# A fused attention and feed-forward block: six of eight W1 blocks by seven products, and a new order of work around them

## The chip, the cores and the metric

The kernel runs on one core of one Trainium2 chip. The core has five engines, each with its own queue that it works through in order: TensorE (PE in the profile; PEld is its weight loads, which run beside its matmuls), VectorE (DVE), ScalarE (ACT), GpSimd (POOL) and SyncE (SP), which here only issues DMAs. The metric is the device time of one launch in microseconds (us): 1520.04 us, the median of three runs (1518.93 to 1522.97).

## The reference

Everything is float32. With x and ctx of shape (128 batches, 128 positions, 256 features), 16 heads of 16 features and a hidden layer of 1024:

```python
q = heads(x @ Wq + bq); k = heads(ctx @ Wk + bk); v = heads(ctx @ Wv + bv)
scores = q @ k^T / 4, and -1e30 where key position >= query position
attn = softmax(scores); the first query's row is zero
x1 = layer_norm(x + merge(attn @ v) @ Wo + bo) * ln1_g + ln1_b
out = layer_norm(x1 + relu(x1 @ W1 + b1) @ W2 + b2) * ln2_g + ln2_b
```

W1 is 256 x 1024 and W2 is 1024 x 256. The two of them are what the change is about.

## The kernel before, in words

Batches are worked in 64 pairs, numbered p. The program is written out in full, with no loop on the chip, and the order of the instructions in the source is the order in each engine's queue; a framework adds the semaphores. After some opening pairs (functions `third` to `sixth`) there are 57 calls of `step(p)`, for p = 7 to 63. One step holds work of several pairs at once: the weighing of the values for pair p-2, the scores and the softmax of pair p, the projections of pair p+1, the first norm of pair p-2, the W1 layer of pair p-3, the W2 layer of pair p-4 and the second norm of pair p-5. All steps but the last (56 of them) have the W1 layer done by `hidden_by_seven`.

"By seven" is a Strassen-like scheme: a product of 2 x 2 blocks takes seven block products where the plain way takes eight, and the rest is additions on other engines. `second_by_seven` (the W2 layer) does this for the whole layer: seven products of four matmuls each into two PSUM banks, py (bank 6) and pz (bank 7), with `empty`, which puts NOPs on TensorE's queue, after each matmul. `sum_of_seven` adds them on VectorE. `combine_hidden` (GpSimd, lines 795 to 798) makes the sums hS of hidden blocks that three of the products need.

For W1 the class `Hidden` does it for the first 2*NI of the eight blocks of 128 hidden units. NI is 2: four blocks by seven products (`run`, line 899, numbers 1 to 7), each of NI matmuls of 128 columns. Each product fills half a PSUM bank of 512 words; two share a bank (`WHERE`). The other four blocks are plain: `plain` (line 938), two matmuls of 256 columns for each. `combine_normed` (GpSimd, lines 866 to 869) makes the sums xS of the normed input, and `combine_w1` those of the weights, once.

The seven products become hidden blocks like this: `keep` (ACT, line 908) copies product 1, `u2` (DVE, line 911) adds 6, `u3` (lines 914 and 915) adds 7 and then 4, and `rest` adds 5 to all odd blocks (line 919) and 2 and 3 to the low halves (line 923). Then `relu` (ACT, line 928) works on each block, in place for those by seven and out of PSUM for the plain ones. Of the four in-place ones, blocks 2 and 3 are done at the head of the next step.

Other lines that matter: `weigh` (PE, lines 494 and 504, bank 7) opens a step, and `context` (ACT, line 516) copies its result out. `scores_both` (PE, line 384) follows and writes all eight banks; its last two groups go to banks 6 and 7, and its high part to banks 0 to 3. `mask` and `mask_high` (DVE, lines 398, 754, 758) find the maxima, `exponential_by_head` (ACT, line 775) does 32 exponentials. Then come `queries` (bank 4, copied at line 272), `attention_out` (bank 5, added at line 549), `keys` (bank 0, copied at line 291) and `values` (bank 1, copied by `spread_values`, line 315, and `stack_values`, line 324). `norm1` is line 565 and `norm2` line 602, both on ACT. `sums` takes reciprocals on DVE (line 433) and multiplies on GpSimd (line 434). `turn` (DVE, line 447) transposes a third of the softmax in blocks of 32, `bring` (SP, line 462) moves the blocks by 16 DMAs. `turn_x1` (DVE, line 674, and five DMAs) transposes x1. `deviation` and `shift` are small GpSimd operations (lines 543, 544, 588), `residual1` (lines 577, 580) and `finish` (lines 608, 609) larger ones.

Of the kernel before, what the change touches and what calls it, by code (L numbers as in the profile page):

```python
# [10 lines left out]
ALU = mybir.AluOpType  # L11
AX = mybir.AxisListType

P = 128
# [5 lines left out]
def tile_cross_attention_block(  # L20
# [22 lines left out]
    nc = tc.nc  # L43
# [30 lines left out]
    states = {}  # L74
# [135 lines left out]
    def at_bank(i, name):  # L210
        return psum.tile([P, 512], F32, tag=f"b{i}", name=name)
# [229 lines left out]
    def turn(p, hi, t):  # L441

        st = states[p]
        if "tb" not in st:
            st["tb"] = wide(f"tb_{p}").rearrange("p (j n) -> p j n", j=NS)
        at = (t if hi else 2) * 256
        nc.vector.transpose(  # L447
            st["tb"][:, :, at : at + 256].rearrange("p j (n a) -> p n j a", a=32),
            st["sm", hi].rearrange("p h j -> p (h j)")[:, t * 1024 : (t + 1) * 1024].rearrange(
                "p (n j a) -> p n j a", j=NS, a=32  # L450
            ),
        )
# [100 lines left out]
    def attention_stats(p):  # L553
        stats(p, states[p]["t1"], 1)
        deviation(p, 1)
# [42 lines left out]
    def norm2(p):  # L598
        st = states[p]
        t2, sd, nb = st["t2"], st["sd", 2], st["nb", 2]  # L600
        for s in range(2):
            nc.scalar.activation(
                t2[:, s], t2[:, s], AF.Identity, bias=nb[:, s], scale=sd[:, s]
            )
# [195 lines left out]
    def second_by_seven(p):  # L800

        st = states[p]
        hT, hs = st["hT"], st["hS"]
        py = st["py"] = at_bank(6, f"py_{p}")
        pz = st["pz"] = at_bank(7, f"pz_{p}")

        def product(out, left, right, after):
            for k in range(FC // 2):
                nc.tensor.matmul(  # L809
                    out, left(k), right(k), start=(k == 0), stop=(k == FC // 2 - 1)  # L810
                )
                empty(after // (FC // 2) + (after % (FC // 2) > k))

        def raw(e, s):
            return lambda k: hT[:, 2 * k + e, s * P : (s + 1) * P]

        def weights(e, h):
            return lambda k: w2[:, 2 * k + e, h * P : (h + 1) * P]

        product(py[:, :P], raw(0, 0), weights(0, 0), 7)  # L820
        product(pz[:, :P], raw(1, 0), weights(1, 0), 7)
        product(pz[:, 2 * P : 3 * P], raw(1, 1), lambda k: wt[:, 3, k], 7)
        product(py[:, 3 * P :], lambda k: hs[:, 0, k], lambda k: wt[:, 0, k], 7)
        product(py[:, 2 * P : 3 * P], lambda k: hs[:, 2, k], lambda k: wt[:, 2, k], 7)
        product(py[:, P : 2 * P], lambda k: hs[:, 1, k], lambda k: wt[:, 1, k], 7)
        product(pz[:, P : 2 * P], lambda k: hs[:, 3, k], weights(1, 1), 6)

    def sum_of_seven(p):

# [17 lines left out]
            t[:, :3], t[:, :3], pz[:, : 3 * P].rearrange("p (n d) -> p n d", d=P), ALU.add  # L847
        )

    NI = 2  # L850
    w1t = const.tile([P, 4, NI, P], F32, tag="w1t", name="w1t")

    def combine_w1():
# [7 lines left out]
    def combine_normed(p):  # L861

        st = states[p]
        x1T = st["x1T"]
        xs = st["xS"] = ffn.tile([P, 4, NS, 32], F32, tag="xS", name=f"xS_{p}", bufs=1)
        nc.gpsimd.tensor_tensor(xs[:, 0], x1T[:, 1, :, 0, :], x1T[:, 1, :, 1, :], ALU.add)
        nc.gpsimd.tensor_tensor(xs[:, 2], x1T[:, 0, :, 0, :], x1T[:, 1, :, 0, :], ALU.subtract)
        nc.gpsimd.tensor_tensor(xs[:, 1], xs[:, 0], x1T[:, 0, :, 0, :], ALU.subtract)
        nc.gpsimd.tensor_tensor(xs[:, 3], x1T[:, 0, :, 1, :], xs[:, 1], ALU.subtract)

    class Hidden:

        WHERE = {1: (2, 0), 6: (2, 1), 7: (3, 0), 4: (3, 1), 2: (4, 0), 3: (4, 1), 5: (5, 0)}

        def __init__(self, p):
            st = states[p]
# [2 lines left out]
            self.h = self.hT[:, : 2 * NI].rearrange("p (i e) (s t) -> p e s i t", e=2, s=2)  # L879
            self.banks, self.plains = {}, {}  # L880

        def of(self, which, n=1):
            at, n0 = self.WHERE[which]
            if at not in self.banks:
                self.banks[at] = at_bank(at, f"phs_{self.p}_{at}")
            return self.banks[at][:, n0 * NI * P : (n0 + n) * NI * P]

        def run(self, which):
            raw = lambda s, k: self.x1T[:, s, :, k, :]
# [24 lines left out]
            nc.vector.tensor_tensor(self.h[:, 1, 1], self.h[:, 1, 0], self.one(7), ALU.add)  # L914
            nc.vector.tensor_tensor(self.h[:, 0, 1], self.h[:, 1, 1], self.one(4), ALU.add)

        def rest(self):
            odd = self.hT[:, 1 : 2 * NI : 2].rearrange("p i (s t) -> p i s t", s=2)
            nc.vector.tensor_tensor(
                odd, odd, self.one(5)[:, :, None, :].to_broadcast([P, NI, 2, P]), ALU.add  # L920
            )
            low = self.h[:, :, 0]
            nc.vector.tensor_tensor(
                low, low, self.of(2, 2).rearrange("p (e i t) -> p e i t", e=2, i=NI), ALU.add
            )

        def relu(self, f):
# [395 lines left out]
    def hidden_by_seven(p):  # L1323

        h = Hidden(p - 3)
        h.run(1)
        h.run(6)
        h.keep()
        stack_values(p)
        h.u2()  # L1330
        h.run(7)
        h.run(4)
        h.u3()
        h.run(2)
        h.run(3)
        h.run(5)
        h.rest()
        norm2(p - 5)
        h.plain([4], 0)
        h.relu(4)  # L1340
        h.plain([5], 1)
        h.relu(5)
        h.plain([6], 2)
        h.relu(6)
        turn(p, 1, 1)
        h.plain([7], 0)
        h.relu(7)
        for f in range(NI):
            h.relu(f)
        states[p - 3]["rest"] = h  # L1350

    def step(p):
        last = p == NP - 1
        weigh(p - 2)
        context(p - 2)
        if p > 7:
            for f in range(NI, 2 * NI):
                states[p - 4]["rest"].relu(f)
        scores_both(p)
        combine_hidden(p - 4, POOL_ALONE)  # L1360
        add_bo(p - 1)
        if not last:
            combine_normed(p - 3)
            load_ahead(p)
        mask(p, 0, B)
        if last:
            mask(p, 0, A)
        mask_high(p, A)
        exponential_by_head(p, 1, ONES, True)
        mask_high(p, B)  # L1370
        exponential_by_head(p, 1, TWOS, True)
        if not last:
            mask(p, 0, A)
        low_maximum(p)
        if not last:
            exponential_by_head(p, 0, range(H), True)
            queries(p + 1)
        attention_out(p - 2)
        attention_sum(p - 2)
        attention_stats(p - 2)  # L1380
        shift(p - 2, 1)
        if last:
            values(p)
            values_out(p)
            stats(p - 5, states[p - 5]["t2"], 2)
            deviation(p - 5, 2)
            norm1(p - 2)
            exponential_by_head(p, 0, range(H), True)
        else:
            norm1(p - 2)  # L1390
            keys(p + 1)
            values(p)
        sums(p, 1, ONE)
        sums(p, 1, TWO)
        if p + 2 < NP:
            tokens(p + 2, "x")
            tokens(p + 2, "c")
        if last:
            shift(p - 5, 2)
            turn_x1(p - 2)  # L1400
        else:
            stats(p - 5, states[p - 5]["t2"], 2)
            scale_and_shift(p - 5)
        turn(p, 1, 0)
        second_by_seven(p - 4)
        if not last:
            sums(p, 0, ALL)
        residual1(p - 3)
        sum_of_seven(p - 4)
        if last:  # L1410
            sums(p, 0, ALL)
        if not last:
            turn_x1(p - 2)
            spread_values(p)
            hidden_by_seven(p)
        else:
            turn(p, 1, 1)
            hidden(p - 3, range(FC))
        turn(p, 0, 0)
# [15 lines left out]
    def behind(p):  # L1435

        weigh(p)
        context(p)
        if p == NP - 2:
            norm2(p - 4)  # L1440
            finish(p - 4)
            store(p - 4)
            bring(p + 1, nc.scalar, LATE_FIRST[len(EVERY) // 2 :])
        combine_hidden(p - 2, VECTOR_ALONE)
        if p == NP - 2:
            stats(p - 3, states[p - 3]["t2"], 2)
            scale_and_shift(p - 3)
        norm2(p - 3)
        finish(p - 3)
        store(p - 3)  # L1450
        second_by_seven(p - 2)
        attention_out(p)
        attention_sum(p)
        attention_stats(p)
        shift(p, 1)
        residual1(p - 1)
        sum_of_seven(p - 2)
        stats(p - 2, states[p - 2]["t2"], 2)
# [75 lines left out]
```

## Time and profile before

| what | value |
|---|---|
| median of three runs | 1520.04 us |
| the profiled execution, its own time | 1522.34 us |
| its span | 1520.5 us |
| granted TensorE clock | 0.998 |
| TensorE matmuls busy | 99% |
| weight loads / VectorE / ScalarE / GpSimd busy | 89% / 84% / 85% / 89% |

The rows of the timeline read: start in us, length in us, engine, line, operation, tile written <- tiles read, shape, how many were merged, and in brackets how long the engine sat idle before and what ended that. Every float32 matmul of the source shows as two records. The record of a matmul begins before the one ahead of it has ended, so that the spacing of starts tells its cost. A row of the windows view has the stretch, its length, and the busy time and instruction count of each engine in it.

### The profile page before, as it was taken

The page shows a single profiled execution, that of the slowest core. Times are in us where ns is not written, and L with a number is a line of the kernel's source. Part 1 is how long each engine was busy: PE and PEld are TensorE (multiplying, and loading weights), DVE is VectorE, ACT ScalarE, POOL GpSimd, SP SyncE. Part 2 cuts the span into 40 slices and gives each one's busy share as a digit, 9 for nine tenths or more (in the row PEclk, how much of TensorE's full clock was granted, in tenths as well). Part 3 has the DMA queues.
Part 4 walks back from the last instruction along what each step waited for, and adds up shares of the span by engine and source line. Part 5 has one row for each costly group of instructions (what it writes and reads, how often), then busy time and mean ns, then how long its engine had stood idle before and what let it go on. Part 6 is the DMA issues. An engine that isn't in the chain of part 4 may idle for free.

```text
span 1520.5 us, 53525 instructions
## 1 busy us (share of the span) xinstructions
PE 1506.5 (99%) x18598; PEld 1359.2 (89%) x18598; DVE 1281.6 (84%) x2607; ACT 1295.0 (85%) x5271; POOL 1358.2 (89%) x1510
## 2 busy tenths in 40 slices
PE   8999999999999999999999999999999999999998
PEld 7788998999999989989989999899899899999987
DVE  7989888888888888888888888888888888888775
ACT  5668988988988989989889889899899898898862
POOL 6878999999999999999999999999999999999983
PEclk9999999999999999999999999999999999999999
DMA  9456665655655656656566566556565666664441
GB/s 196 91 113 144 147 151 139 138 133 135 141 142 138 131 140 135 147 138 135 134 137 142 141 140 129 142 133 150 134 140 131 139 137 146 138 132 124 108 119 47
DMA packets 415314, 204.59 MB, mean 135 GB/s; under 512 B 282448, under 2 KB 383056, under 8 KB 415056
## 3 DMA queue, kind: packets, MB, share of 16 engines
q1 hardware_dynamic: 412768, 199.34, 56.9%
q8 instruction: 158, 2.59, 0.8%
q10 hardware_dynamic: 2288, 1.85, 0.5%
q14 instruction: 100, 0.82, 0.2%
HBM read 70.26 MB, written 33.29 MB: 68 GB/s over the span
## 4 chain that ended last, share of the span: by engine, by line
PE 92%; DVE 3%; ACT 2%; POOL 1%; DMA 1%; SPq 1%; issue 1%; ACTq 0%; POOLq 0%; DVEq 0%
PE ph L938 13%; PE py L809 13%; PE phs L899 11%; PE pz L809 10%; PE pq L261 7%; PE po L523 7%; PE pv L301 7%; PE pk L261 6%; PE pss L384 6%; PE pc L504 4%; PE ph L710 3%; PE pc L494 2%; ACT sm L775 1%; SPq L462 1%; POOL sm L434 1%
## 5 line engine op out<-in xcount | busy, mean ns | idle before, releaser
L775 ACT ACTIVATE sm<-pss,nmx 128x128 f32<-128x128 f32 x944 | 328.5, 405 | 87.1 <-POOL hS L795 74.9
L434 POOL TENSOR_TENSOR sm<-sm,rs 128x1024 f32<-128x1024 f32 x192 | 362.1, 1900 | 3.4 <-DVE rs L433 3.3
L447 DVE STREAM_TRANSPOSE tb<-sm 128x1024 f32<-128x1024 f32 x186 | 223.4, 1226 | 110.9 <-POOL sm L434 90.7
L775 ACT ACTIVATE sm<-sm,nmx 128x64 f32<-128x64 f32 x944 | 313.7, 404 | 0.0
L775 ACT ACTIVATION_READ_ACCUMULATOR sm<-sm,nmx 128x1 f32 x912 | 235.1, 258 | 0.0
L775 ACT ACTIVATION_READ_ACCUMULATOR sm<-pss,nmx 128x1 f32 x912 | 223.3, 245 | 0.0
L938 PE MATMUL ph<-x1T,w 128*128 128x256 f32 x896 | 213.8, 386 | 0.1
L938 PEld LDWEIGHTS ph<-x1T,w 128*128 128x128 f32 x896 | 161.3, 190 | 36.1 <-ACT vd L324 18.8
L809 PE MATMUL py<-wt,hS 128*128 128x128 f32 x1440 | 171.2, 275 | 1.0 <-DVE hS L796 0.5
L809 PEld LDWEIGHTS py<-wt,hS 128*128 128x128 f32 x1440 | 165.8, 192 | 1.4 <-DVE hS L796 0.7
L758 DVE TENSOR_REDUCE nmx<-pss 128x4 f32<-128x512 f32 x236 | 150.9, 680 | 0.0
L398 DVE TENSOR_TENSOR sm<-pss,neg 128x256 f32<-128x256 f32 (+1 forms) x276 | 108.3, 435 | 34.9 <-PE pss L384 32.0
L928 ACT ACTIVATE hT<-ph,b1e_c 128x256 f32<-128x256 f32 x224 | 98.8, 465 | 35.5 <-PE ph L938 35.5
L291 ACT ACTIVATE kT<-pk,bkh,half 128x256 f32<-128x256 f32 x252 | 123.7, 609 | 4.0 <-PE pk L261 4.0
L261 PE MATMUL pq<-xT,wq 128*128 128x256 f32 x504 | 125.4, 392 | 0.5 <-DVE sm L398 0.5
L523 PE MATMUL po<-wo,cxT 128*128 128x256 f32 x512 | 121.3, 380 | 0.7 <-ACT cxT L516 0.7
L301 PE MATMUL pv<-wv,cT 128*128 128x256 f32 x512 | 120.9, 379 | 0.0
L261 PE MATMUL pk<-cT,wk 128*128 128x256 f32 x504 | 119.2, 379 | 0.0
L795 POOL TENSOR_TENSOR hS<-hT 128x512 f32<-128x512 f32 x57 | 72.2, 1267 | 50.2 <-ACT hT L928 50.1
L523 PEld LDWEIGHTS po<-wo,cxT 128*128 128x128 f32 x512 | 96.9, 190 | 14.4 <-ACT cxT L516 1.2
L261 PEld LDWEIGHTS pq<-xT,wq 128*128 128x128 f32 x504 | 90.7, 189 | 20.8 <-issue 9.8
L301 PEld LDWEIGHTS pv<-wv,cT 128*128 128x128 f32 x512 | 97.2, 190 | 13.2
(164 smaller groups left out, 3987.4 us busy)
## 6 DMA issues: line engine op xcount, KB each, us to landing
pT<-tb SPq DMA_DIRECT2D x976, 96.0 KB, 2.2
x1t<-tbx SPq DMA_DIRECT2D x252, 64.0 KB, 1.8
x1T<-x1t SPq DMA_DIRECT2D x63, 256.0 KB, 2.9
out_dram<-t SPq DMA_DIRECT2D x63, 256.0 KB, 2.4
xb<-in_x_dram SPq DMA_DIRECT2D x124, 128.0 KB, 3.8
cb<-in_ctx_dram SPq DMA_DIRECT2D x124, 128.0 KB, 3.8
x<-in_x_dram SPq DMA_DIRECT2D x31, 512.0 KB, 4.6
w<-in_L_xattn_W_dram SPq DMA_DIRECT2D x2, 1024.0 KB, 7.7
```

What stands on the lines that cost most here:

```text
L261: nc.tensor.matmul(ps[:, m * TP : (m + 1) * TP], w[:, k, m * P : (m + 1) * P], src[:, k, :], start=(k == 0), stop=(k == KC - 1),)
L291: nc.scalar.activation(st["kT"][:, m, e, :], pk[:, m * TP : (m + 1) * TP], AF.Identity, bias=bkh[:, m, e : e + 1], scale=half[:, e : e + 1],)
L301: nc.tensor.matmul(pv[:, s * D : (s + 1) * D], st["cT"][:, k, s * P : (s + 1) * P], wv[:, k, :], start=(k == 0), stop=(k == KC - 1),)
L398: nc.vector.tensor_tensor(st["sm", hi][:, 4 * r : 4 * r + 4, :], st["sps", hi][r][:, : 4 * n].rearrange("p (n j) -> p n j", j=n), no[:, No ...
L434: nc.gpsimd.tensor_tensor(sm[:, part, :], sm[:, part, :], rs[:, :, None].to_broadcast([P, part.stop - part.start, n]), ALU.mult,)
L447: nc.vector.transpose(st["tb"][:, :, at : at + 256].rearrange("p j (n a) -> p n j a", a=32), st["sm", hi].rearrange("p h j -> p (h j)")[:, ...
L523: nc.tensor.matmul(po[:, s * D : (s + 1) * D], cxT[:, k, s, :], wo[:, k, :], start=(k == 0), stop=(k == KC - 1),)
L758: nc.vector.tensor_reduce(st["nmx", 1][:, 4 * r : 4 * r + 4], st["sps", 1][r].rearrange("p (n j) -> p n j", j=P), AX.X, ALU.max, negate=True,)
L775: nc.scalar.activation(sm[:, h, :], src, AF.Exp, bias=nmx[:, h : h + 1], scale=1.0, **({"accum_out": st["su", hi][:, h : h + 1]} if summed ...
L809: nc.tensor.matmul(out, left(k), right(k), start=(k == 0), stop=(k == FC // 2 - 1))
L899: nc.tensor.matmul(ps[:, i * P : (i + 1) * P].rearrange("p (n a) -> p n a", a=32), left(i), right, start=True, stop=True,)
L938: nc.tensor.matmul(self.plains[f].rearrange("p (s i a) -> p s i a", s=2, a=32), w1[:, k, f * P : (f + 1) * P], self.x1T[:, :, :, k, :], st ...
```

## The change

1. NI goes from 2 to 3: six of the eight W1 blocks are done by seven products, each of three matmuls of 128 columns, and only blocks 6 and 7 are plain. Each of the seven products has a bank of its own (banks 2, 3, 4, 5, 6, 0, 1), and the plain blocks reuse banks 2 and 3.
2. `rest` is split into `add2`, `add3` and `add5`, placed apart. The relus run in the order 0, 2, 4, 6, 1, 7, and 3 and 5 at the head of the next step. `norm1` moves behind `u3`, and the W1 function takes over `turn_x1`, which stood ahead of it.
3. On GpSimd the two high softmax products come first; `combine_normed`, `deviation` and `shift` of the first norm stand behind them.
4. On VectorE the second high transpose, which stood among the W1 work, moves to directly behind the first, ahead of the W2 sum.
5. The NOPs among the W2 matmuls become 5 for a product (4 for the last) in place of 7 (6).
6. In the closing pairs, `finish` and `store` of one pair move behind other GpSimd work.

```diff
-        product(py[:, :P], raw(0, 0), weights(0, 0), 7)
+        product(py[:, :P], raw(0, 0), weights(0, 0), 5)
...
-        product(pz[:, P : 2 * P], lambda k: hs[:, 3, k], weights(1, 1), 6)
+        product(pz[:, P : 2 * P], lambda k: hs[:, 3, k], weights(1, 1), 4)
...
-    NI = 2
+    NI = 3
...
-        WHERE = {1: (2, 0), 6: (2, 1), 7: (3, 0), 4: (3, 1), 2: (4, 0), 3: (4, 1), 5: (5, 0)}
+        WHERE = {1: 2, 6: 3, 7: 4, 4: 5, 2: 6, 3: 0, 5: 1}
...
-        def rest(self):
+        def add2(self):
+            nc.vector.tensor_tensor(self.h[:, 0, 0], self.h[:, 0, 0], self.one(2), ALU.add)
+
+        def add3(self):
+            nc.vector.tensor_tensor(self.h[:, 1, 0], self.h[:, 1, 0], self.one(3), ALU.add)
+
+        def add5(self):
             odd = self.hT[:, 1 : 2 * NI : 2].rearrange("p i (s t) -> p i s t", s=2)
             nc.vector.tensor_tensor(
                 odd, odd, self.one(5)[:, :, None, :].to_broadcast([P, NI, 2, P]), ALU.add
-            )
-            low = self.h[:, :, 0]
-            nc.vector.tensor_tensor(
-                low, low, self.of(2, 2).rearrange("p (e i t) -> p e i t", e=2, i=NI), ALU.add
             )
...
         h.u3()
+        norm1(p - 2)
         h.run(2)
+        h.add2()
         h.run(3)
         h.run(5)
-        h.rest()
-        norm2(p - 5)
-        h.plain([4], 0)
+        h.relu(0)
+        h.relu(2)
         h.relu(4)
-        h.plain([5], 1)
-        h.relu(5)
+        h.add3()
+        h.add5()
         h.plain([6], 2)
         h.relu(6)
-        turn(p, 1, 1)
-        h.plain([7], 0)
+        turn_x1(p - 2)
+        h.plain([7], 3)
+        norm2(p - 5)
+        h.relu(1)
         h.relu(7)
-        for f in range(NI):
-            h.relu(f)
...
         if p > 7:
-            for f in range(NI, 2 * NI):
-                states[p - 4]["rest"].relu(f)
+            states[p - 4]["rest"].relu(3)
+            states[p - 4]["rest"].relu(5)
...
         if not last:
-            combine_normed(p - 3)
             load_ahead(p)
...
-        attention_stats(p - 2)
-        shift(p - 2, 1)
+        stats(p - 2, states[p - 2]["t1"], 1)
...
-            norm1(p - 2)
             keys(p + 1)
             values(p)
         sums(p, 1, ONE)
         sums(p, 1, TWO)
+        if not last:
+            combine_normed(p - 3)
+            deviation(p - 2, 1)
+            shift(p - 2, 1)
...
         turn(p, 1, 0)
+        if not last:
+            turn(p, 1, 1)
         second_by_seven(p - 4)
...
-            turn_x1(p - 2)
             spread_values(p)
             hidden_by_seven(p)
...
         if p == NP - 2:
             norm2(p - 4)
-            finish(p - 4)
-            store(p - 4)
             bring(p + 1, nc.scalar, LATE_FIRST[len(EVERY) // 2 :])
         combine_hidden(p - 2, VECTOR_ALONE)
         if p == NP - 2:
             stats(p - 3, states[p - 3]["t2"], 2)
             scale_and_shift(p - 3)
+            finish(p - 4)
+            store(p - 4)
```

More of the change, by code (lines that the diff above doesn't have):

```diff
@@ L818, in weights @@
             return lambda k: w2[:, 2 * k + e, h * P : (h + 1) * P]
-        product(py[:, :P], raw(0, 0), weights(0, 0), 7)
[L821 to L825, printed above, removed]
-        product(pz[:, P : 2 * P], lambda k: hs[:, 3, k], weights(1, 1), 6)
+        product(py[:, :P], raw(0, 0), weights(0, 0), 5)
+        product(pz[:, :P], raw(1, 0), weights(1, 0), 5)
+        product(pz[:, 2 * P : 3 * P], raw(1, 1), lambda k: wt[:, 3, k], 5)
+        product(py[:, 3 * P :], lambda k: hs[:, 0, k], lambda k: wt[:, 0, k], 5)
+        product(py[:, 2 * P : 3 * P], lambda k: hs[:, 2, k], lambda k: wt[:, 2, k], 5)
+        product(py[:, P : 2 * P], lambda k: hs[:, 1, k], lambda k: wt[:, 1, k], 5)
+        product(pz[:, P : 2 * P], lambda k: hs[:, 3, k], weights(1, 1), 4)
     def sum_of_seven(p):
@@ L880, in __init__, with of @@
             self.banks, self.plains = {}, {}
[L882 to L886, printed above, removed]
+        def of(self, which):
+            if which not in self.banks:
+                self.banks[which] = at_bank(self.WHERE[which], f"phs_{self.p}_{which}")
+            return self.banks[which][:, : NI * P]
         def run(self, which):
@@ L1394, in step @@
         sums(p, 1, TWO)
+        if not last:
+            combine_normed(p - 3)
+            deviation(p - 2, 1)
+            shift(p - 2, 1)
         if p + 2 < NP:
```

## The prediction

> **What bounds the kernel now.** I read the page's head and its chain, then the windows view for the length of a step, then each engine's timeline through one step.
>
> ```profile
> span 1520.5 us, 53525 instructions
> PE 1506.5 (99%) x18598; PEld 1359.2 (89%) x18598; DVE 1281.6 (84%) x2607; ACT 1295.0 (85%) x5271; POOL 1358.2 (89%) x1510
> PE 92%; DVE 3%; ACT 2%; POOL 1%; DMA 1%; SPq 1%; issue 1%; ACTq 0%; POOLq 0%; DVEq 0%
> 235.10:1439.70 1204.60, 1204.48 (x15185) 1095.66 (x15184) 1027.83 (x2131) 1083.70 (x4576) 1113.29 (x1249) 1.00 0.59 137
> L911 DVE TENSOR_TENSOR hT<-hT,phs 128x256 f32<-128x256 f32 x56 | 23.6, 422 | 13.9 <-ACT hT L908 13.9
> L838 DVE TENSOR_TENSOR t<-t,py 128x384 f32<-128x384 f32 x60 | 33.3, 554 | 2.1
> ```
>
> TensorE is 92% of the chain. The stretch from 235.10 to 1439.70 us, from one step's weighing to another's 52 steps later, gives 1204.60/52 = 23.165 us a step; `u2` (L911) runs once in each step that changes: 56. So 0.1 us a step is 5.6 us of the whole. TensorE's own step:
>
> ```profile
> 768.09 0.43 PE L494 MATMUL pc<-pT,vd 128*32 128x64 f32 x16
> 769.57 1.62 PE L384 MATMUL pss<-kT,qT 32*64 32x128 f32 x64
> 771.12 1.99 PE L261 MATMUL pq<-xT,wq 128*128 128x256 f32 x8
> 776.40 1.89 PE L301 MATMUL pv<-wv,cT 128*128 128x256 f32 x8
> 778.13 1.05 PE L809 MATMUL py<-w,hT 128*128 128x128 f32 x8
> 784.38 0.61 PE L899 MATMUL phs<-x1T,w 128*128 128x128 f32 x4
> 787.50 3.82 PE L938 MATMUL ph<-x1T,w 128*128 128x256 f32 x16
> 788.46 2.46 PEld L938 LDWEIGHTS ph<-x1T,w 128*128 128x128 f32 x12 [0.33 <-ACT vd L324]
> 791.25 0.43 PE L494 MATMUL pc<-pT,vd 128*32 128x64 f32 x16
> ```
>
> By starts, eight records of 256 columns take 778.13-776.40 = 1.73, 0.216 each. The 56 of 128 columns in the W2 layer take 784.38-778.13 = 6.25, 0.1116 each, and the 28 of W1's seven products 787.50-784.38 = 3.12, the same. The plain blocks' 16 take 3.75 where 16 x 0.216 = 3.46: 0.29 over, most of it the wait for `stack_values` (vd), which frees bank 1.
>
> **The change on TensorE.** A step loses 28 records of 128 and 16 of 256 columns (3.12+3.75 = 6.87) and gets 42 and 8: 42 x 0.1116 + 8 x 0.216 = 4.69+1.73 = 6.42. The difference is 0.45 if all of the 0.29 goes, 0.16 if all stays. The wait goes if vd is early (below); I give 0.20 of the 0.29 to it and leave 0.09 for the turn to the small loads of the weighing. So 0.36, and a step of 23.16-0.36 = 22.80. The 14 NOPs taken out cost nothing now, for W2 with them has the spacing of W1 without.
>
> ```profile
> L899 PEld LDWEIGHTS phs<-xS,w1t 128*128 128x128 f32 x672 | 84.0, 192 | 0.0
> ```
>
> The Trainium skill (TensorE: Matmul & The Clock Gate, section Back-to-back issue gap) says that in a stream of load and multiply pairs the spacing at 128 columns is set by both, about 81 ns a pass where the multiply alone has 56. An estimate from that page would make our record, at 0.1116 two of its passes, 0.162 and the swap 14 x 0.162 - 8 x 0.216 = 0.54 dearer. The trace disagrees: 0.1116 for 28 in a row.
>
> **Will the others keep up?** I pass the new order through the queues by hand. The clock is zero at the weighing (768.09), so product 1 starts at 784.38-768.09 = 16.29.
>
> ```profile
> 769.71 0.58 ACT L516 COPY cxT<-pc 128x508 f32<-128x508 f32 x1 [0.23 <-PE pc L504]
> 770.18 0.91 ACT L928 ACTIVATE hT<-hT,b1e_c 128x256 f32<-128x256 f32 x2
> 772.51 0.37 ACT L775 ACTIVATE sm<-pss,nmx 128x128 f32<-128x128 f32 x1 [1.42 <-POOL hS L795]
> 783.31 0.87 ACT L272 ACTIVATE qT<-pq,bqs_c 128x256 f32<-128x256 f32 x2
> 784.03 1.14 ACT L565 ACTIVATE x<-t,nb,sd 128x256 f32<-128x256 f32 x2
> 785.01 1.97 ACT L291 ACTIVATE kT<-pk,bkh,half 128x256 f32<-128x256 f32 x4
> 786.81 0.69 ACT L315 COPY vz<-pv 128x256 f32<-128x256 f32 x2
> 787.32 0.44 ACT L908 COPY hT<-phs 128x256 f32<-128x256 f32 x1
> 787.59 0.82 ACT L324 COPY vd<-pv 64x256 f32<-64x256 f32 x2
> 788.44 1.09 ACT L602 ACTIVATE t<-t,nb,sd 128x256 f32<-128x256 f32 x2
> 789.43 0.82 ACT L928 ACTIVATE hT<-ph,b1e_c 128x256 f32<-128x256 f32 x2
> ```
>
> ACT: the exponentials start at 4.42 after VectorE's first maximum and end at 15.22, as before. qT to 15.94, kT (1.80) to 17.74, vz to 18.25; `norm1` (0.98) no longer stands between. `keep`, half wider, is through at 18.80 (0.44 and some 0.1), vd at 19.5. Product 5, which needs vd's bank now, starts at 16.29 + 6 x 0.67 = 20.3: that wait is gone. `norm1` ends at 20.5, and ACT waits for `add2`.
>
> ```profile
> 770.37 0.76 DVE L398 TENSOR_TENSOR sm<-pss,neg 128x256 f32<-128x256 f32 x2 [0.52 <-PE pss L384]
> 778.49 0.24 DVE L433 RECIPROCAL rs<-sa 128x8 f32<-128x8 f32 x2
> 780.76 0.18 DVE L537 BATCH_NORM_AGGREGATE mv<-bs 128x2 f32<-128x6 f32 x1
> 782.85 1.25 DVE L447 STREAM_TRANSPOSE tb<-sm 128x1024 f32<-128x1024 f32 x1 [1.90 <-POOL sm L434]
> 784.15 0.63 DVE L838 TENSOR_TENSOR t<-x1b,py 128x512 f32<-128x512 f32 x1
> 786.85 0.70 DVE L674 STREAM_TRANSPOSE tbx<-x 128x512 f32<-128x512 f32 x1
> 787.80 0.42 DVE L911 TENSOR_TENSOR hT<-hT,phs 128x256 f32<-128x256 f32 x1 [0.25 <-ACT hT L908]
> 788.33 0.42 DVE L914 TENSOR_TENSOR hT<-hT,phs 128x256 f32<-128x256 f32 x1
> 780.92 3.75 POOL L434 TENSOR_TENSOR sm<-sm,rs 128x1024 f32<-128x1024 f32 x2
> 776.20 1.28 POOL L254 TENSOR_TENSOR xb<-x,bov_r 128x512 f32<-128x512 f32 x1
> 771.17 1.27 POOL L795 TENSOR_TENSOR hS<-hT 128x512 f32<-128x512 f32 x1 [0.89 <-ACT hT L928]
> ```
>
> POOL does the same work as before; its one wait is 0.89, so it needs 23.16-0.89 = 22.27 a step and still fits. The high products can't start before the reciprocals (778.49, done at 10.64), so POOL gets a wait of some 0.5 there, and ends them at 12.5 and 14.4, not 14.7 and 16.6. `combine_normed` behind them ends at 16.3; product 6, the first to need it, starts at 17.0. `shift` ends at 17.9, ahead of `norm1` at 19.5; `finish` at 26.6, which is 3.8 in the next step, so hS moves from 3.08 to 3.8, and W2 needs its first sum only at 12.7.
>
> DVE: its wait of 1.90 shrinks; the transposes run at 12.8 and 14.4 and end at 15.6, the W2 sum (784.15 to 786.85, 2.7) runs from 15.7 to 18.4. The adds are a half wider: 0.55 by L838 for 0.42. So DVE gets 3 x 0.13 in `u2` and `u3` and about 0.7 for the three late adds, some 1.1 a step, in place of the 1.9. `u2` waits for `keep` (18.8), then 0.66 to each `u3` (0.53 now, plus 0.13; the second has a TensorE wait of its own now), and `add2` ends between 21.2 and 21.4; `add3` and `add5` end at 22.7, the x1 transpose at 23.3, the low one at 24.5, which is 1.7 in the next step; the mask (2.28) is not delayed. `turn_x1` is 3.8 later than now (786.85-768.09 = 18.76 to 22.6) and pushes its five DMAs, the store and `bring` back on SP by about 2; x1T is needed a step later at 14.4 and pT at its end, so nothing waits.
>
> ACT again: in-place relus space at 0.41 (770.18), those from PSUM at 0.36, `norm2` 0.99. From `add2`: 3 x 0.41 + 0.36 + 0.99 + 0.41 + 0.36 = 3.35. So ACT is free for `context` at 21.35+3.35 = 24.70. A weighing that starts at 22.80 wants it 1.62 later (769.71-768.09): 24.42. That is the new wait: 0.28 late.
>
> ```profile
> L384 PEld LDWEIGHTS pss<-kT,qT 32*64 32x64 f32 x3840 | 81.3, 131 | 8.8 <-ACT hT L718 1.2 <-ACT cxT L516 0.5
> ```
>
> The row has one wait of the scores for that copy. Their last two groups write bank 7, which it empties. The scores take 771.12-769.57 = 1.55; each pair of strips does two groups of 256 and two of 128 columns, so the third is due 0.43+0.11 before the end, at about 770.5; the copy ends at 770.29 and the load takes 0.13. The slack is between nothing and 0.1. I take nothing: 0.28 late is then 0.28 on TensorE, but a longer step gives ACT as much time back, so that half of it stays: 0.14 a step (between 0 and 0.28). The step: 22.80+0.14 = 22.94.
>
> The sum: 56 x (23.165-22.94) = 12.6 us. `combine_w1`, run once, gets half longer, under 1 us of POOL, ahead of the steps; the closing pairs' reorder takes `finish` out of the way of `scale_and_shift` on POOL there and moves a store on SP: between -1 and +1, taken as 0. Against the profiled execution's 1522.3 (2.3 above the median of the runs) that is 1509.7; from the median, 1520.0-12.6, about 1508.
>
> **The rivals.**
>
> *TensorE alone.* If `add2` is 0.3 sooner, or the scores have the slack, the step is 22.80: 56 x 0.365 = 20 less, 1500. For it: 1.42 of ACT's idle time ahead of the exponentials. Against: `context` stands ahead of that idle time.
>
> *The gain is eaten.* If ACT's run from `add2` to `context` is 0.4 longer, 25.1, the step is 22.80 + (25.1-24.42)/2 = 23.14: 1519.
>
> *Slower: the late adds wait for the relus.* `add3` and `add5` write the odd blocks, which lie between the even ones that relus 0, 2 and 4 write just before. If the semaphores guard the whole stretch, `add3` waits for relu 4 (22.7); `add5` then ends at 24.3 and the low transpose at 26.1, and with the mask at 2.28 behind it the loop closes only at a step of 23.8: 56 x 0.64 = 36 more, 1556. It decides once `add3` starts over 0.6 late. Against: relu 4 (789.43) ran while `rest` was writing blocks of the same tile, so the tile as a whole isn't guarded; no pair of interleaved writes stands in this trace.
>
> *Slower: code loading.*
>
> ```profile
> q8 instruction: 158, 2.59, 0.8%
> ```
>
> These are blocks of 16.4 KB; a step's TensorE code has 14 NOPs less and 12 matmul and load records more, so it may lie differently across the blocks. Without a wait of that kind in this step's rows I bound it by 0.33, the load wait above: 18 more than forecast, 1526. The Trainium skill (Runtime: NRT & Kernel Launch, section Instruction fetch mechanics) calls crossing a block mostly hidden; the trace so far agrees.
>
> *Weight loads bind.* If each record of 128 columns took its load's 192 ns, 14 x 0.192 - 8 x 0.216 = 0.96 more a step: 54 more, 1574. The spacing of 0.1116 excludes it nearly.
>
> **How the numbers follow.** Forecast 0.43, TensorE alone 0.25, eaten 0.12, late adds 0.10, code or something unseen 0.09, weight loads 0.01. A change of 0.3% (4.6 us, about what a measurement can tell) parts the first two, 0.68, from eaten, 0.12, and the last three, 0.20. The likeliest's own range, with 0 to 0.28 for the new wait and 0.16 to 0.45 for the swap, is 1500 to 1516; the range reaches to 1498 and 1525, taking in TensorE alone and the eaten gain, and leaves out the slower ones.
>
> **What would show it.** Right: the spacing of 0.1116 in 42 records; no wait for vd; steps of 22.8 to 23.0, perhaps a short and a long one by turns, as a late step gives ACT time; a wait of the scores for cxT; ACT idle before relu 0; DVE's wait for POOL's products under 1 us. Wrong: `add3` waiting for ACT, the mask starting late, TensorE waiting inside the products, or a wait for "issue" among them.

## The result and the profile after

The changed kernel takes **1501.99 us** (median of 4 runs, 1501.28 to 1502.62) against 1519.59 us for the kernel before (four runs beside these, 1518.93 to 1522.97): a ratio of 0.988, with a 95% interval of 0.9863 to 0.9897. The prediction was 1508 us in a range of 1498 to 1525. The profiled execution of after took 1501.94 us.

The page's head and its code queue, of the kernel after:

```profile
span 1500.2 us, 53576 instructions
PE 1487.9 (99%) x18934; PEld 1366.7 (91%) x18934; DVE 1334.8 (89%) x2663; ACT 1290.5 (86%) x5271; POOL 1357.8 (91%) x1510
q8 instruction: 158, 2.59, 0.8%
PE 93%; DVE 3%; POOL 2%; DMA 1%; issue 1%; ACT 1%; SPq 0%; ACTq 0%; POOLq 0%; DVEq 0%
```

TensorE still carries the chain, 93%. The same 52 steps in the windows view (the stretch, its length, then each engine's busy time and count):

```profile
235.18:1420.82 1185.64, 1185.64 (x15497) 1102.30 (x15496) 1079.03 (x2183) 1080.08 (x4578) 1112.92 (x1249) 1.00 0.60 139
```

1185.64/52 = **22.801 us a step**, where before had 23.165. This is to the hundredth the step of the rival "TensorE alone" (22.80), and not the 22.94 of the forecast. TensorE's timeline through one step (columns as before):

```profile
782.40 0.43 PE L494 MATMUL pc<-pT,vd 128*32 128x64 f32 x16
783.88 1.62 PE L384 MATMUL pss<-kT,qT 32*64 32x128 f32 x64
785.42 1.99 PE L261 MATMUL pq<-xT,wq 128*128 128x256 f32 x8
798.69 0.83 PE L898 MATMUL phs<-x1T,w 128*128 128x128 f32 x6
...
803.38 1.89 PE L939 MATMUL ph<-x1T,w 128*128 128x256 f32 x8
805.20 0.43 PE L494 MATMUL pc<-pT,vd 128*32 128x64 f32 x16
```

The 42 records of the seven products take 803.38-798.69 = 4.69 us, 0.1117 each, and the 8 plain ones 805.20-803.38 = 1.82: together 6.51 for 6.87, which is the predicted 0.36. No row carries a wait, and the wait for `stack_values` (vd) is gone. The other engines in the same step, ACT first:

```profile
800.63 0.56 ACT L907 COPY hT<-phs 128x384 f32<-128x384 f32 x1
801.00 0.82 ACT L324 COPY vd<-pv 64x256 f32<-64x256 f32 x2
801.84 1.09 ACT L565 ACTIVATE x<-t,nb,sd 128x256 f32<-128x256 f32 x2
803.60 1.31 ACT L929 ACTIVATE hT<-hT,b1e_c 128x256 f32<-128x256 f32 x3 [0.66 <-DVE hT L917]
806.91 0.56 ACT L516 COPY cxT<-pc 128x508 f32<-128x508 f32 x1
```

VectorE and GpSimd in that step:

```profile
795.47 2.60 DVE L447 STREAM_TRANSPOSE tb<-sm 128x1024 f32<-128x1024 f32 x2 [0.22 <-DMA pT<-tb]
801.23 0.56 DVE L910 TENSOR_TENSOR hT<-hT,phs 128x384 f32<-128x384 f32 x1 [0.32 <-ACT hT L907]
803.01 0.55 DVE L917 TENSOR_TENSOR hT<-hT,phs 128x384 f32<-128x384 f32 x1
803.48 0.55 DVE L920 TENSOR_TENSOR hT<-hT,phs 128x384 f32<-128x384 f32 x1
805.00 0.70 DVE L674 STREAM_TRANSPOSE tbx<-x 128x512 f32<-128x512 f32 x1
805.63 1.20 DVE L447 STREAM_TRANSPOSE tb<-sm 128x1024 f32<-128x1024 f32 x1
786.19 1.27 POOL L795 TENSOR_TENSOR hS<-hT 128x512 f32<-128x512 f32 x1
793.03 3.75 POOL L434 TENSOR_TENSOR sm<-sm,rs 128x1024 f32<-128x1024 f32 x2 [0.53 <-DVE rs L433]
```

From the weighing at 782.40: `add2` (L917) starts at 20.61, the relus behind it at 21.20, `add3` (L920) at 21.08 while the three relus run, and `context` (L516) at 24.51, which is 1.71 into the next step. GpSimd waits 0.53 for the reciprocals, and hS starts at 3.79.

Where the 20.3 us between the two spans come from, by the starts of the weighings: the 56 changed steps are 19.9 us shorter (1297.2 to 1277.3), the start-up is 1.0 longer, the closing interval between the last two weighings 1.6 shorter (18.22 to 16.64), the end behind it 0.2 longer. The medians differ by 17.6, less than that, because the profiled execution of before, 1522.34, was itself 2.7 us over that median.

### The profile page after: what moved, and what is told of

It reads as the page before. It is cut to its first block, busy times and chain, and to the rows that moved or that the text cites. A ratio compares the mean times of both kernels' runs of the same rounds, so it can differ in the third digit from the quotient of the medians.

```text
span 1500.2 us, 53576 instructions
## 1 busy us (share of the span) xinstructions
PE 1487.9 (99%) x18934; PEld 1366.7 (91%) x18934; DVE 1334.8 (89%) x2663; ACT 1290.5 (86%) x5271; POOL 1357.8 (91%) x1510
## 3 DMA queue, kind: packets, MB, share of 16 engines
q8 instruction: 158, 2.59, 0.8%
## 4 chain that ended last, share of the span: by engine, by line
PE 93%; DVE 3%; POOL 2%; DMA 1%; issue 1%; ACT 1%; SPq 0%; ACTq 0%; POOLq 0%; DVEq 0%
PE phs L898 18%; PE py L809 14%; PE pz L809 10%; PE pq L261 8%; PE pv L301 7%; PE po L523 7%; PE pk L261 7%; PE ph L939 6%; PE pss L384 6%; PE pc L504 4%; PE pc L494 2%; PE ph L710 2%; POOL sm L434 1%; PE py L730 0%; DVE sm L398 0%
## 5 line engine op out<-in xcount | busy, mean ns | idle before, releaser
L447 DVE STREAM_TRANSPOSE tb<-sm 128x1024 f32<-128x1024 f32 x186 | 228.1, 1229 | 22.4 <-POOL sm L434 12.0
L775 ACT ACTIVATION_READ_ACCUMULATOR sm<-sm,nmx 128x1 f32 x912 | 231.8, 254 | 0.0
L929 ACT ACTIVATE hT<-hT,b1e_c 128x256 f32<-128x256 f32 x336 | 152.1, 501 | 37.0 <-DVE hT L917 37.0
L898 PE MATMUL phs<-xS,w1t 128*128 128x128 f32 x1008 | 130.9, 275 | 0.0
L898 PEld LDWEIGHTS phs<-xS,w1t 128*128 128x128 f32 x1008 | 121.6, 192 | 0.0
L261 PEld LDWEIGHTS pk<-cT,wk 128*128 128x128 f32 x504 | 95.7, 190 | 13.1 <-issue 0.2
```

What stands on the lines that cost most here:

```text
L261: nc.tensor.matmul(ps[:, m * TP : (m + 1) * TP], w[:, k, m * P : (m + 1) * P], src[:, k, :], start=(k == 0), stop=(k == KC - 1),)
L447: nc.vector.transpose(st["tb"][:, :, at : at + 256].rearrange("p j (n a) -> p n j a", a=32), st["sm", hi].rearrange("p h j -> p (h j)")[:, ...
L775: nc.scalar.activation(sm[:, h, :], src, AF.Exp, bias=nmx[:, h : h + 1], scale=1.0, **({"accum_out": st["su", hi][:, h : h + 1]} if summed ...
L898: nc.tensor.matmul(ps[:, i * P : (i + 1) * P].rearrange("p (n a) -> p n a", a=32), left(i), right, start=True, stop=True,)
L929: nc.scalar.activation(self.hT[:, f], self.plains.get(f, self.hT[:, f]), AF.Relu, bias=b1e_c[:, f : f + 1], scale=1.0,)
```

## The experiments

A step's length below is the distance of two starts of `pc` (line 494) in the trace; 56 such distances lie in the changed stretch.

**Only `norm1` and `turn_x1` moved, in the kernel before.**

```diff
-            norm1(p - 2)
             keys(p + 1)
...
         h.u3()
+        norm1(p - 2)
...
         h.relu(6)
+        turn_x1(p - 2)
         turn(p, 1, 1)
```

> The kernel before with the first norm moved behind u3 and the x1 transpose behind relu 6, nothing else. If the wait for vd cost TensorE 0.20 us a step, the step is 22.96 and the time 56 x 0.20 = 11 us below the kernel before, about 1508. If it cost the whole 0.29 that the plain blocks were over: 16 us less, 1504. If another wait takes its place: 1520.

Measured: 1511.76 us, ratio 0.9934 (0.9917 to 0.995), a step of 22.963 for 23.161. That is 0.198 less, and no wait for vd is left in the steps: the 0.20 that the prediction gave to this wait. So more than half of the step's gain of 0.36 comes from two moved lines, without any change of the products. From 22.963 to the 22.801 of after remain 0.162: the plain swap of 16 records of 256 columns for 14 of 128, predicted as 0.16. So the two terms of the sum on TensorE hold one by one.

**Two blocks of each half by seven (NI of 2), in the changed order with a bank for each product.**

```diff
-    NI = 3
+    NI = 2
```

The plain blocks 4 to 7 go to banks 2 to 5, and relus 1 and 3 to the next step's head.

> The changed kernel with NI back at 2: four blocks by seven, each product in its own bank, four plain blocks in banks 2 to 5; all else stays. Column count: a step has 28 records of 128 and 16 of 256 columns for 42 and 8, 6.58 us for 6.42, so 22.96 us for 22.80 and 56 x 0.16 = 9 us more than the changed kernel, about 1511. Rival, that the order alone makes the gain: the time of the changed kernel, 1502. Rival, that the swap makes all of it: 1520.

Measured: 1541.88 us, ratio 1.0127 (1.0112 to 1.0142), a step of 23.46. The expectation (22.96) missed. The waits view, for TensorE's loads and its matmuls (total us, times, longest):

```profile
PEld phs L898 <- ACT vd L324: 20.8, 50, 0.4
PE phs L898 <- ACT vd L324: 11.3, 49, 0.2
```

The wait for vd is back, now at product 5. With two matmuls a product it comes at 16.29 + 6 x 0.446 = 18.97, ahead of vd at about 19.4; with three it came at 20.3. So the larger NI isn't only the cheaper swap: its longer products are the cover under which bank 1 comes free. Own banks and the smaller NI together are slower than the kernel before.

**ACT made late on purpose**, by one or two copies of a finished block ahead of `context` (0.30 us each on ACT).

```diff
         h.relu(7)
+        for f in (6, 4)[:1]:     # [:2] in the second kernel
+            nc.scalar.copy(h.hT[:, f], h.hT[:, f])
```

> The changed kernel with one more ACT operation a step, a copy of a finished hidden block on itself (256 columns, some 0.35 to 0.41 us) right ahead of the context copy. If ACT's lateness there comes through to TensorE by half beyond a slack of 0.1 us, as the prediction had it: the step grows by some 0.15, 8 us more than the changed kernel, about 1510. If it comes through whole: 0.35, some 20 us, 1522. If ACT's idle time before the exponentials takes it up: 1502.

> The same with two such copies a step. By half: some 0.35 us a step, 20 us more than the changed kernel, 1522. Whole: 0.75, 42 us more, 1544. Taken up: 1502.

Measured: 1507.44 us (0.9904, 0.989 to 0.9919) with one copy, 1517.38 (0.9967, 0.9955 to 0.9979) with two. The steps alternate, as predicted for a late `context`. With two copies the waits view of TensorE's loads names it, in about every second step:

```profile
PEld pss L384 <- ACT cxT L516: 7.2, 30, 0.5
```

With one copy it names no wait for cxT, and the lateness is read from the starts. Three weighings in a row on TensorE with one copy, and the two `context` copies between them on ACT:

```profile
783.24 0.43 PE L494 MATMUL pc<-pT,vd 128*32 128x64 f32 x16
806.08 0.43 PE L494 MATMUL pc<-pT,vd 128*32 128x64 f32 x16
829.07 0.43 PE L494 MATMUL pc<-pT,vd 128*32 128x64 f32 x16
...
785.08 0.58 ACT L516 COPY cxT<-pc 128x508 f32<-128x508 f32 x1
808.07 0.58 ACT L516 COPY cxT<-pc 128x508 f32<-128x508 f32 x1
```

`context` at 1.84 gives a step of 22.84, at 1.99 one of 22.99. With two copies:

```profile
790.61 0.43 PE L494 MATMUL pc<-pT,vd 128*32 128x64 f32 x16
813.57 0.43 PE L494 MATMUL pc<-pT,vd 128*32 128x64 f32 x16
836.78 0.43 PE L494 MATMUL pc<-pT,vd 128*32 128x64 f32 x16
...
792.57 0.58 ACT L516 COPY cxT<-pc 128x508 f32<-128x508 f32 x1
815.79 0.58 ACT L516 COPY cxT<-pc 128x508 f32<-128x508 f32 x1
```

At 1.96 it gives 22.96, at 2.22 one of 23.21. All four points lie on one line: 22.80 and whatever `context` starts behind 1.80. So do the other steps of both kernels behind their first changed one, 110 in all, each within 0.02 us; the earliest `context` among them, at 1.80, has a step of 22.80. So the limit is 1.80, not the 1.62 at which it started before: a slack of 0.18, where the prediction took none out of 0 to 0.1. And the rule "a late step gives ACT the time back" holds: with one copy 1.84 + 0.19 and 1.99 + 0.04 make the same 2.03, so that lateness is shared between two steps and half of it counts.

**The second high transpose back among the W1 work**, the rest as after.

```diff
         turn(p, 1, 0)
-        if not last:
-            turn(p, 1, 1)
...
         h.relu(6)
+        turn(p, 1, 1)
         turn_x1(p - 2)
```

> The changed kernel with the second high transpose back among the W1 work, behind relu 6. VectorE does it after add5 then; by the trace of the changed kernel the low transpose ends 1.17 us later, at 25.6 us after the weighing, and the mask, 2.28 after the next weighing, has to wait: the loop closes at a step of 23.35, 0.55 x 56 = 31 us more than the changed kernel, about 1533. Rival, that VectorE's place doesn't matter while TensorE bounds: 1502.

Measured: 1520.01 us (0.9994, 0.9985 to 1.0004), a step of 23.13: without this part nothing is left of the gain. VectorE's timeline:

```profile
790.56 1.24 DVE L447 STREAM_TRANSPOSE tb<-sm 128x1024 f32<-128x1024 f32 x1
792.31 1.20 DVE L447 STREAM_TRANSPOSE tb<-sm 128x1024 f32<-128x1024 f32 x1
793.44 0.72 DVE L398 TENSOR_TENSOR sm<-pss,neg 128x256 f32<-128x256 f32 x2
```

The waits of TensorE's loads in the same kernel:

```profile
PEld pq L261 <- DVE sm L398: 21.2, 57, 0.4
```

The extra transpose pushes the low one and, behind it, the mask from 2.28 to 793.44-790.51 = 2.93, and the queries, which write a bank that the mask reads, wait for it in 57 steps. The size was off (0.33 a step for the 0.55 expected), the place right.

**GpSimd's order of before** (`combine_normed` early, `deviation` and `shift` ahead of the softmax products), the rest as after.

```diff
         add_bo(p - 1)
         if not last:
+            combine_normed(p - 3)
             load_ahead(p)
...
         stats(p - 2, states[p - 2]["t1"], 1)
+        deviation(p - 2, 1)
+        shift(p - 2, 1)
...
         sums(p, 1, TWO)
-        if not last:
-            combine_normed(p - 3)
-            deviation(p - 2, 1)
-            shift(p - 2, 1)
```

> The changed kernel with combine_normed, deviation and shift back ahead of the high softmax products. The second product ends 3.5 us later, the second high transpose waits for it, and the W2 sum, u2, u3, add2, the relus, the context copy, relus 3 and 5 and hS follow in one loop that I add up to 24.6 us: 1.8 x 56 = 100 us more than the changed kernel, about 1600. Rival, that GpSimd's order was worth only what VectorE waited for it before (1.9 us, beside other work): 1502.

Measured: 1637.32 us, ratio 1.0767 (1.0749 to 1.0785), a step of 25.22 where 24.6 was expected: the loop was found, its length was taken too short. TensorE's timeline at product 2:

```profile
820.48 0.91 PE L898 MATMUL phs<-x1T,w 128*128 128x128 f32 x6 [1.80 <-DVE t L838]
```

Its waits over the span:

```profile
PE phs L898 <- DVE t L838: 100.7, 56, 1.8
```

Both high transposes now stand ahead of the W2 sum (line 838) and wait for GpSimd's products; the sum is late by that, and product 2 needs the sum's bank 6. The two moves belong together: the transposes may go ahead of the sum only because GpSimd's products come first.

**All eight blocks by seven** (NI of 4, no plain block; `norm2` earlier, and x1b with two buffers for three, for room).

```diff
-    NI = 3
+    NI = 4
```

> The same idea once more: NI = 4, all eight blocks by seven, no plain ones, the second norm moved ahead of the relus, and two buffers in place of three for x1b to make room. TensorE alone: 56 records of 128 columns for 42 and 8 of 256, 6.25 us for 6.42, so 22.63 a step, 9.5 us less than the changed kernel, 1492. VectorE's loop from the mask to the low transpose, with the adds a third wider, I add up to 23.2 us: 0.4 x 56 = 22 more than the changed kernel, 1524. I expect the second.

Measured: 1526.61 us, ratio 1.0039 (1.0024 to 1.0054): slower than before by 0.4%, as expected, but not for the expected reason alone. Its waits of TensorE's loads:

```profile
PEld pq L261 <- DVE sm L398: 26.0, 48, 0.6
PEld pss L384 <- issue: 13.7, 13, 1.8
```

The base step of 23.05 ends at VectorE's mask, which stands behind wider adds: 0.25 a step over the kernel after, 14 us in 56 steps, where 0.4 a step was expected. Some long steps add 11.6 us more in the profiled execution; less these, the time would be about 1515, below the kernel before. So the time near the expected 1524 is in part luck; the second row is the subject of the next four runs.

**The NOPs.** The prediction costed the 14 NOPs taken out at nothing. TensorE's queue, counted in the programs, has 640 instructions a step in both kernels: 292 matmul records, as many loads, 48 NOPs and 8 waits before, and 298, 298, 34 and 10 after. Four kernels change only the number or place of NOPs: after without any (606 a step), after with all 34 in the first two of W2's products (640), after with the 48 of before (654), and before with the 34 of after (626).

```diff
-        product(py[:, :P], raw(0, 0), weights(0, 0), 5)
+        product(py[:, :P], raw(0, 0), weights(0, 0), 0)   # 17, 7 and 5 in the others
```

> The changed kernel without any NOP in the W2 layer: 34 instructions a step less on TensorE's queue. If they are hidden behind the matmuls: 1502, within 2 us. If the way the code lies across its blocks matters, a wait in some of the steps: up to 18 us more, 1520.

> The changed kernel with its 34 NOPs of a step all in the first two of the W2 layer's seven products (17 and 17, then none) instead of 5 by 5; TensorE's queue still has 640 instructions a step, two and a half code blocks of 256. If the long steps of the kernel without NOPs come from where the blocks end (the count per step), this one has the block ends in the same two places of a step as the changed kernel, moved by no more than some 20 instructions within the W2 layer: a step of 22.80 and 1502 to 1503 us, no long steps. If the NOPs help by their spacing between the matmuls, five products without them lose what the kernel without NOPs lost: long steps, mean 22.95, about 1510. If a bunch of NOPs costs time of its own (17 at some 10 to 20 ns that no matmul covers), up to 0.3 a step: up to 1519.

> The changed kernel with the 7 (last 6) NOPs a product of before: 48 a step instead of 34, so 654 instructions a step. Count per step: the block ends drift by 14 instructions a step and pass the dense small matmuls of the weighing and the scores in part of the 56 steps: some 10 to 16 long steps of 0.2 to 1.4 us, 1507 to 1513. Spacing, or NOPs that cost nothing: 1502.

> The kernel before with the 5 (last 4) NOPs a product of after: 626 instructions a step instead of 640, nothing else changed. Count per step: long steps of 0.2 to 1.4 us in some 10 to 16 of the 56 again, so 1525 to 1531. NOPs that cost nothing, as the prediction had it: 1520, as before.

| kernel | instructions a step | time, us | ratio to before | base step | long steps of 56 |
|---|---|---|---|---|---|
| after | 640 | 1501.99 | 0.988 (0.9863 to 0.9897) | 22.80 | 1 |
| all NOPs in front | 640 | 1503.34 | 0.9884 (0.9868 to 0.9901) | 22.80 | 1 |
| no NOPs | 606 | 1511.70 | 0.9941 (0.9927 to 0.9956) | 22.80 | 13 |
| after, 48 NOPs | 654 | 1510.25 | 0.9935 (0.9913 to 0.9956) | 22.80 | 12 |
| before, 34 NOPs | 626 | 1533.54 | 1.0084 (1.0069 to 1.0099) | 23.14 | 19 |
| NI of 2, from above | 628 | 1541.88 | 1.0127 (1.0112 to 1.0142) | 23.46 | 4 |
| NI of 4, from above | 652 | 1526.61 | 1.0039 (1.0024 to 1.0054) | 23.05 | 14 |

A step counts as long from 0.08 us over the middle one; the kernel before has two, of 0.13. Whether a NOP stands between the matmuls doesn't matter, and 17 of them in a product (four or five behind each matmul of the source) cost nothing. The number in a step does: 640 is two and a half times 256, and with any other number tried some steps are longer, nearly all by up to 1.4 us. In the kernel of 626 the times came above the expected 1525 to 1531. In the kernel of before with 34 NOPs, the scores of the longest step on TensorE's timeline:

```profile
959.79 1.58 PE L384 MATMUL pss<-kT,qT 32*64 32x128 f32 x63
962.60 0.32 PE L384 MATMUL pss<-kT,qT 32*64 32x128 f32 x1 [1.23 <-issue]
```

The waits of that kernel, loads and matmuls:

```profile
PEld pss L384 <- issue: 9.7, 14, 1.5
PE pss L384 <- issue: 4.5, 6, 1.2
```

The wait is for "issue", nothing that the profile shows, and it lies among the scores: in this kernel 12.6 us are added between the first score and the first query, and the 56 steps are 11.7 us longer in all than as many middle ones; without NOPs it is 9.0 of 9.8. The code queue on the pages of two kernels, 34 NOPs in the kernel before and no NOPs:

```profile
q8 instruction: 155, 2.54, 0.7%
q8 instruction: 150, 2.46, 0.7%
```

After and before have 158 blocks. The W2 layer runs 60 times, so 14 NOPs less are 840 instructions, and three blocks are missing; 34 NOPs less are 2040 instructions, and eight are missing: 255 to a block (2.59 MB/158 = 16.4 KB, 64 bytes an instruction). So q8 carries TensorE's code. A drift of 14 a step brings a block's end back to the same place each 128/14 = 9 steps where a step holds two and a half blocks, and the nine longest steps of this kernel stand in two rows of that distance: the 14th, 23rd, 41st and 50th, and the 18th, 27th, 36th, 45th and 54th. That the place of the blocks' ends decides is shown by these runs.

That the next block isn't there in time is shown by their traces, when TensorE's queue is counted through (loads, matmuls, NOPs and waits in their order) and laid beside the times of q8's packets. In the five kernels without 640 instructions a step, the loads stop 52 times for "issue", for over 0.2 us, among the scores or behind them. All 52 stops stand at the same place: an instruction whose number, from the first of the queue in the trace, is 193 modulo 256. So that is taken for the place where a block begins. Each stop ends 1.20 to 1.66 us after a packet of q8 has landed. In none of the kernels does a block begin sooner than 1.20 us after the landing of its packet. In the nine kernels with 640 no such stop occurs, and none of their blocks is through in under 4.33 us. Weighing and scores put 160 matmul records and 160 loads, 1.25 blocks, into 3.0 us: a block that begins near the start of a weighing is through in 2.0 to 2.5 us, and then the next has to be there. What sets the 1.20 us, and when a packet starts, is open. So is whether 640 with the blocks' ends in other places would be as free of stops; no run tried it.

**The closing pairs' `finish` back in its old place**, the rest as after.

```diff
             norm2(p - 4)
+            finish(p - 4)
+            store(p - 4)
...
             scale_and_shift(p - 3)
-            finish(p - 4)
-            store(p - 4)
```

> The changed kernel with the closing pairs' finish and store of one pair back where they stood before, the other parts kept. In the profile of the changed kernel the closing interval between the last two weighings but the final one is 16.64 us, before it was 18.22, with two waits of TensorE of 0.52 for VectorE's hS sums while finish ran on GpSimd. If the place of finish is what does it: 18.2 for the interval, the two waits are back, some 1.6 us more, 1503.5 us. If something else of the change does it (the prediction took the reorder as 0): 16.64 and 1502.

Measured: 1501.79 us, ratio 0.987 (0.9853 to 0.9886), against 0.988 for after: no difference that can be measured, though the interval is back at 18.19 us. On its timeline `finish` on GpSimd runs beside VectorE's hS sums, and TensorE waits for these (twice, once shown):

```profile
1443.92 0.65 DVE L795 TENSOR_TENSOR hS<-hT 128x512 f32<-128x512 f32 x1
1443.91 1.79 POOL L608 TENSOR_TENSOR t<-t,g_r 128x512 f32<-128x512 f32 x1
1444.49 1.76 DVE L796 TENSOR_TENSOR hS<-hT 128x512 f32<-128x512 f32 x1
1446.31 1.16 PE L809 MATMUL py<-wt,hS 128*128 128x128 f32 x8 [0.52 <-DVE hS L796]
```

In the kernel after, the same sum with GpSimd idle:

```profile
1444.82 0.68 DVE L796 TENSOR_TENSOR hS<-hT 128x512 f32<-128x512 f32 x1
```

So the place of `finish` makes the interval 1.6 us longer; 0.5 of that comes back behind the last weighing (42.37 for 42.85), and the rest is within what single runs differ by. Of the total, this edit has at most 1.6.

## Why the prediction was right, and where it was off

- **TensorE's swap** (42 x 0.1116 + 8 x 0.216, less 0.09 for the turn to the small loads): right. 6.51 for the 6.42 + 0.09. The two terms were measured apart, 0.198 and 0.162. That 0.20 of the 0.29 would go was a choice, which no row of the prediction gives; that it came out so closely is in part luck. The rule of the Trainium skill (TensorE: Matmul & The Clock Gate, section Back-to-back issue gap), by which the record would cost 0.162, disagrees with 4.69/42 = 0.1117, and the rival on weight loads falls with it.
- **The new wait, 0.14 a step:** this step failed. In the changed kernel the wait isn't there at all, so the likeliest course of the prediction (0.43) did not happen; what happened is its rival "TensorE alone" (0.25), which the range took in. The prediction had `context` 0.28 late, without slack: it took the 1.62 at which the copy starts once the weighing is done for the latest time at which it may start. It was wrong at both ends: `add2` starts at 20.61 and frees relu 0 at 21.20, not 21.35, the run behind it takes 3.31 us for 3.35, so `context` comes at 24.51 for 24.70; and it may come as late as 1.80 into a step, 24.60 at this length, not 24.42. So it is 0.09 early, and nothing is lost. The slack could be had from the prediction's own rows: 771.12 less 0.43 and 0.11 is 770.58, not "about 770.5", which leaves 0.16 ahead of the load, near the 0.18 measured. The mechanism stands: the two kernels with ACT made late show the alternation and the half, and with two copies the wait for cxT. This term is 56 x 0.14 = 7.8 us, more than the 6 us by which the forecast was too high.
- **The sums:** the forecast's own sum, 1520.0-12.6, is 1507.4 and was given as 1508. The likeliest's own range of 1500 to 1516 holds the swap at 0.36; with 0.16 to 0.45 for it, as the text says, it would be 1495 to 1527, wider than the whole range given.
- **ACT's and VectorE's pass:** vd no longer waited for, u2 at 18.83 (18.8 predicted), ACT idle 0.66 ahead of relu 0, the mask where it was (2.28). `turn_x1` starts at 22.60, as predicted, and nothing waits for its DMAs. The low transpose starts at 23.23 and ends at 24.43 (24.5).
- **GpSimd's pass:** the wait for the reciprocals is 0.53 (0.5), hS starts at 3.79 (3.8), and the second product ends at 14.38 (14.4). VectorE's transposes wait for them no longer in this step (1.90 before).
- **The late adds wait for the relus** (rival): no. `add3` (803.48 to 804.03) and the three relus (803.60 to 804.91) ran at the same time, and the low transpose was not late.
- **The gain is eaten** (rival): no, by 0.1 us. With two copies on ACT (0.60) all but 5 us of it are eaten, by the mechanism that this rival named.
- **NOPs cost nothing:** right for this change, but by luck, for a reason that the prediction didn't have. The 14 NOPs less and the 12 records and 2 waits more leave 640 a step. With 654, the change would have come to 1510.
- **Code loading** (rival, 1526): it didn't come, but it is real. The bound of 0.33 a step wasn't far: the mean over all steps is 0.17 to 0.24 in the three kernels with another number of NOPs, though a single step mostly loses up to 1.4. The Trainium skill (Runtime: NRT & Kernel Launch, section Instruction fetch mechanics) calls a block's end mostly hidden; the prediction let the trace agree, and the kernels with 606, 626 and 654 instructions a step disagree, by 8 to 13 us.
- **Closing pairs, -1 to +1, taken as 0:** no change in the total could be measured, though the interval lost 1.6 for a cause that the prediction didn't name (VectorE and GpSimd beside each other).

## What to carry to other kernels

A late wait that sits at an engine's turn from step to step costs half of its size, and its slack is best read from two kernels that are made late on purpose: the point where the line bends is the limit. Before an instruction count is changed on a queue with a dense stretch of small instructions, count the instructions of a step and see where its code blocks begin: a block that begins at the head of the dense stretch is through before the next one is there. A step of a whole or half number of blocks keeps these places fixed, and any edit that adds or removes instructions, NOPs too, lets them drift and can cost more than it brings. Moves that pay together may cost when made alone (the transposes without GpSimd's new order lost 135 us against after), so each needs its partner's cover named.

## What the runs showed of the hardware

- Blocks of 256 instructions (16.4 KB) of TensorE's code: with 640 a step, in the kernel after and the one with all NOPs in front, no step but the first changed one is longer; with 606, 626 or 654 a fifth to a third of them are, mostly by 0.1 to 1.4 us. All 52 stops (the kernels with 628 and 652 among them) stand at the beginning of a block and end 1.20 to 1.66 us after a packet of the code queue has landed. The block size agrees with the Trainium skill (Runtime: NRT & Kernel Launch, section Instruction fetch mechanics); that the crossing is mostly hidden doesn't, in this dense stretch.
- VectorE and GpSimd, each in a sum or product of 128x512 with two inputs, at the same time: 1.76 for 0.68 us and 1.79 for 1.27. The Trainium skill (SBUF — State Buffer, section SBUF: two separate sides) has the two engines share a pair of ports that one of them holds for a whole instruction. The rows fit that, with the two taking turns: GpSimd's product starts 0.66 us before VectorE's sum of line 795 ends and is longer by 0.52. VectorE's next sum, of line 796, ends 0.55 behind GpSimd's product (1446.25 and 1445.70), about as if it had begun only then.
- One step of the kernel with 48 NOPs was 3.66 us longer. After a stop of its loads of 1.83 us at the scores, the windows view of it has TensorE at a granted clock of 0.56 (the value behind the instruction counts) for the 3.4 us that follow:

```profile
216.51:219.90 3.39, 3.39 (x10) 2.74 (x10) 3.36 (x7) 3.39 (x21) 3.31 (x4) 0.56 0.64 201
```

So a stop can cost once more than its own length. It was seen once; stops of 1.79 and 1.72 us in the kernel with NI of 4 had no such drop behind them, and its condition is open.
